# Image 1's backward convolution taps: from the vector engine to products with diagonal matrices on the tensor engine

## The chip, the cores and the metric

The kernel runs on one core of a Trainium2 chip. The metric is the device time of one execution in microseconds (us). A core has a tensor engine (PE in the profile, its weight loads PEld), a vector engine (DVE), a scalar engine (ACT), a general engine (POOL), a queue that issues all transfers here (SP), and 16 DMA engines. The engines run side by side, each through its own list of instructions in order, and wait for one another by semaphores. Everything is in fp32.

## The reference, cut to what matters

Two images of 48 x 48 tokens with 768 channels go through two residual layers. Layer 0 is attention of every token to its 7 x 7 neighbourhood. Layer 1 is a selective scan (Mamba) over the 2304 tokens of an image in both directions:

```
xz = X @ in_proj_w.T                                   # x and z, 1536 channels each
out_f = branch(xz, conv_w, conv_b, ...)                # forward
out_b = branch(xz reversed in time, conv_w_b, ...)     # backward, turned back afterwards
out = (out_f + out_b) @ out_proj_w.T

branch: x = silu(depthwise_conv(x, 4 taps) + conv_b)
        dt, B, C = x @ x_proj_w.T;  delta = softplus(dt @ dt_proj_w.T + b)
        h[t] = exp(delta[t] * A) * h[t-1] + delta[t] * x[t] * B[t]      # 16 states a channel
        y[t] = sum over states of h[t] * C[t] + x[t] * Dp;  result y * silu(z)
```

The depthwise convolution has four taps for each channel: a sum of four shifted copies of the channel's row, each times a number that belongs to the channel. The backward branch takes its taps from the other side, so both branches read the same projected row x, with three more tokens on each side.

## The kernel before, in words

**Layout.** Channels lie on the 128 partitions, time along the free dimension. The 2304 tokens are cut into 6 chunks of 384 (CHUNKS), the 1536 inner channels into ND = 12 blocks of 128. One block in one chunk in one direction is a *unit*; 12 units are a *pass*. There are 24 passes, 288 units: image 0 forward (passes 0 to 5), image 0 backward (6 to 11), image 1 forward (12 to 17), image 1 backward (18 to 23).

**A unit** (scan, from L1180) has four groups of four states. Per group: a product delta*x*B over 4 x 386 elements (L1225, tile hb), which the planner gives to DVE or to POOL for three of the four groups; four exponentials on ACT into PSUM (L1247, tile da); two scans on DVE of two states each (L1258); a product with C on POOL (L1273); transposing products on PE that add the states up (L1290, tile py). ACT then copies py to SBUF (L1316). So a unit has 8 scans and a pass has 96. Before a unit, deltas_of projects delta (L1151, L1157), takes the softplus (L1162), multiplies by Dp (L1170, ACT) and by x (L1175, POOL).

**The projections and the convolution** (in_proj, from L880). For each chunk the normalised inputs xc (six blocks of 128 channels, 390 tokens) are loaded. For each block k of the 1536, u_tile loads 384 KB of weights w_x and makes six products into a PSUM bank px (L382, called from product). From px both branches' convolutions are made, for back = 0 and back = 1: ACT writes the tap that has no shift with the bias (L928), DVE adds the other three taps one after the other (L935), all reading px in PSUM:

```
def tap(j, back=back, q=q, at=at):
    u = uz[:, back, kk, :cl]
    nc.vector.scalar_tensor_tensor(
        u, px[:, at[j] : at[j] + cl], q["conv_w"][:, k, j : j + 1], u,
        ALU.mult, ALU.add,
    )
```

Three blocks are collected in a tile uz, ACT applies silu to them (L961, with a table load ahead and behind), and they are stored. x_proj loads them again and makes dt, B and C.

**What lies beside what.** The attention of image 0 comes first. Its in_proj is spread over image 0's forward passes, the attention of image 1 over units 50 to 118, in_proj of image 1 from unit 118 on, 12 units to a chunk. Its z parts for the first four chunks and the output projections come later.

**What sets the order.** The program is not written out in order. Every piece of work is handed to a planner (class Order) with its engine, an estimated duration, a key (its place in the sequence of units), and the buffers that it reads and writes. The planner walks through time: each engine takes next the piece that can start first by those estimates; pieces of which a key lies over 2.5 units ahead of the oldest unfinished unit wait. Pieces of the scan rank by key, side work (job=True) may be put off where it would delay scans. Products of L1225 with an alternative (alt) go to whichever engine is free first. Where PE would stand idle for over 0.8 us between a unit's first and last transposes, the planner adds transposes of the identity (L1491, called *fillers* here) that nobody reads. Each engine then executes its list in the planned order, whatever the chip does.

**Buffers.** Tag "mm": 2 PSUM banks, shared by px, the delta, z, x_proj and output products and by the last transposes of a backward unit. Tag "w": 5 SBUF buffers for weights. Tag "ev": 4 buffers of 384 columns for copies out of PSUM. Tag "hb": 7 buffers. Loads and stores all go through the SP queue in planned order; a load that waits for its buffer holds up the ones behind it.

Of the kernel before, what the change touches and what calls it, by code (L numbers as in the profile page):

```python
# [48 lines left out]
CONV = 4  # L49
HALO = CONV - 1  # L50
NEG = -1e30

# [193 lines left out]
def tile_kernel(  # L246
# [56 lines left out]
    yg = spill("yg", [DI, L], ND * NCW)  # L303

    state = Buf("state", parts=ND * NSG, ap=res.tile([P, ND, 2 * NS + 1], F32, tag="state", name="state"))
    nc.gpsimd.memset(state.ap, 0.0)
# [15 lines left out]
    def ps(tag, n):  # L322
        return Buf(f"{tag}_{n}", psum, [P, 512], tag, BUFS.get(tag, 1))
# [48 lines left out]
    def product(acc, cl, w, x, key, m=P, job=True, o0=0, to=None, also=()):  # L372
# [4 lines left out]
        for c0 in range(0, n, 3):  # L377

            def part(c0=c0):
# [10 lines left out]
                "PE", mm(3, cl), part, key, [*used, *([] if first else [acc])],  # L390
                [acc, *([to] if first and to else [])], job=job,
            )

    def parameters(key):

        for i, (conv_w, conv_b, xpT, dtT, dt_b, A_log, Dp) in enumerate((fwd, bwd)):
# [18 lines left out]
            add("ACT", 800, decay, key + i + 0.5, r=[v], w=[v], job=True)  # L415
            pars.append(v)
        for j, t in enumerate(xd[0] + xd[1]):

            def unit(t=t):
                for l0, cl in CHUNKS:  # L420
                    nc.sync.dma_start(t.ap[RK : RK + 1, l0 : l0 + cl], ones[:, :cl])

            add("SP", 2400, unit, key + 2 + 0.1 * j, w=[t], job=True)
# [105 lines left out]
    def attention(b, start, end, job, T):  # L529
# [25 lines left out]
        def project(t):  # L555
# [18 lines left out]
            for p in range(NP):  # L574
                for s in range(2):
# [4 lines left out]
                    )  # L580
                    acc, e = ps("mm", f"qk{n}"), sb(turn("ev"), [P, TB], n)
                    product(
# [3 lines left out]
                    if s == 0:  # L586
# [3 lines left out]
                            lambda acc=acc, e=e: nc.scalar.mul(  # L590
                                e.ap.rearrange("p (u r c) -> p u r c", u=HW // QC, r=QR),
                                acc[:, :TB].rearrange("p (r u c) -> p u r c", u=HW // QC, r=QR),
# [5 lines left out]
                    else:  # L598
                        add(
                            "DVE", dve(TB),  # L600
                            lambda acc=acc, e=e: nc.vector.tensor_copy(e.ap, acc[:, :TB]),  # L601
                            key + 0.01, r=[acc], w=[e], **S,
# [4 lines left out]
                    add(  # L607
                        "SP", 400, lambda to=to, e=e: nc.sync.dma_start(to(), e.ap), key + 0.02,
                        r=[e], w=[dst], size=P * TB * 4, **S,
                    )  # L610
            for hf in range(NP // 3):
# [7 lines left out]
                for m in range(TB // P):  # L619
                    n = f"v{b}_{t}_{hf}_{m}"  # L620
                    acc, e = ps("mm", n), sb(turn("ev"), [P, TB], n)
                    for i in range(nw):
# [5 lines left out]
                    add(  # L628
                        "ACT", act(TB), lambda acc=acc, e=e: nc.scalar.copy(e.ap, acc[:, :TB]),
                        key + 0.01, r=[acc], w=[e], **S,  # L630
# [3 lines left out]
                        lambda e=e, m=m, hf=hf: nc.sync.dma_start(  # L634
                            vd[b][t * TB + m * P : t * TB + (m + 1) * P, hf * TB : (hf + 1) * TB], e.ap
                        ),
# [243 lines left out]
    def in_proj(b, i, start, end, conv=True, gate=True, nk=KB, tags=("uz",), banks=("mm",), proj=None):  # L880

        shift, rstd = norms[b]
        l0, cl = CHUNKS[i]
        lo, n = l0 - HALO, cl + 2 * HALO
# [32 lines left out]
        def u_tile(k, kk, nk, uz, key, bank):  # L917
            m = f"{b}_{i}_{k}"
            (wx,) = weights(w_inT, [(0, k * P)], f"x{m}", key, after=got)
            px = ps(bank, f"xin_{m}")  # L920
            product(px, n, [(wx, c, 0) for c in range(NC)], [(xc, c, 0) for c in range(NC)], key, to=uz)
            for back in (0, 1):
                q = par[back]
# [18 lines left out]
                for j in range(HALO):  # L942
                    add(
                        "DVE", dve(cl) + 70, lambda j=j, tap=tap: tap(j), key + 0.04, r=[px, part],
                        w=[part], job=True,
                    )

        def z_tile(k, kk, nk, uz, s, key):
# [83 lines left out]
    def xd_out(b, back, l0, cl, n, acc, key):  # L1032
        t = sb("ev", [P, TB], n)
        add(
# [507 lines left out]
```

## Time and profile before

| what | value |
|---|---|
| median of 6 runs | 7045.02 us (7034.2 to 7048.28) |
| the profiled execution | 7044.31 us; its span in the profile 7042.5 us |
| granted PE clock, mean | 0.978 |
| DMA | 1101.32 MB, mean 156 GB/s |
| L1258 DVE, scans | 2304, 3926.7 us busy |
| L1273 POOL, product with C | 1152, 3654.6 us |
| L1247 ACT, exponentials | 4608, 2677.1 us |
| L1290 PE, transposes | 13824, 1745.1 us |
| L935 DVE, taps, both images | 864 records; the 432 of image 1 between 4015 and 5105 us |
| L928 ACT, first tap with bias | 164.9 us for 264 records on the uz tiles |

How to read it: busy time is the time in which an engine executes; register and semaphore instructions are not counted. In a row of instruction groups stand the line, engine, operation, output tile <- input tiles, shapes and number, then busy us and mean ns of one, then the idle time just before these instructions and what ended most of it. Instructions of one engine can overlap, so busy time divided by the number can be below the mean of one. "uz_u<-mm_xin" is a tile of name uz_u written from a PSUM tile mm_xin. The 40 slices give tenths of busy time along the span. The chain is followed back from the last instruction to whatever released each step.

### The profile page before, as it was taken

The numbers are of one execution on the slowest core, as the hardware profiler recorded it, in microseconds if no ns is written. First come the engines' busy times: TensorE is split into PE (matmuls) and PEld (weight loads), VectorE is DVE, ScalarE is ACT, GpSimd is POOL, SyncE is SP. The second block draws the span as 40 slices with busy tenths as digits, with TensorE's granted clock in tenths as the row PEclk, the third lists the DMA queues.
The fourth block names the chain that finished last, engine by engine and source line by source line (L and its number), as shares of the span: only waits on it lengthen the run. The fifth ranks groups of instructions, "written<-read, shape, count | busy, mean of one in ns | idle before, by whom it ended". The sixth has DMA issues, their size and how long they took to land.

```text
span 7042.5 us, 105645 instructions
## 1 busy us (share of the span) xinstructions
PE 6316.5 (90%) x38151; PEld 4833.1 (69%) x38151; DVE 6062.6 (86%) x6217; ACT 4969.4 (71%) x10948; POOL 5447.3 (77%) x1951
## 2 busy tenths in 40 slices
PE   7999989989999999999988888888888898999888
PEld 5666656666666776676666656666688887777777
DVE  2354449999999999998998999999999999999998
ACT  1323248788888788887888778778876667777765
POOL 0000008888989999998898878999999999999997
PEclk9999989999999999999999999999999999999999
DMA  6565454445556444554444354343466676655553
GB/s 190 173 197 175 137 156 132 141 137 157 156 154 199 152 147 137 156 173 147 128 144 133 112 166 134 100 143 112 141 179 191 176 219 194 194 178 157 162 170 105
DMA packets 1337698, 1101.32 MB, mean 156 GB/s; under 512 B 136328, under 2 KB 1327416, under 8 KB 1337144
## 3 DMA queue, kind: packets, MB, share of 16 engines
q1 hardware_dynamic: 1337176, 1094.56, 51.9%
q8 instruction: 303, 4.96, 0.3%
q14 instruction: 219, 1.79, 0.1%
HBM read 881.41 MB, written 213.57 MB: 155 GB/s over the span
## 4 chain that ended last, share of the span: by engine, by line
DVE 39%; PE 19%; ACT 15%; POOL 13%; issue 9%; DMA 5%; SPq 1%; DVEq 0%; POOLq 0%; ACTq 0%
DVE hb L1258 26%; POOL hb L1273 8%; DVE hb L1225 7%; ACT da L1247 5%; PE mm_qk L382 4%; POOL hb L1225 4%; DVE uz_u L935 3%; PE mm_v L382 2%; PE mm_ao L382 2%; PE py L1290 2%; PE mm_xin L382 1%; ACT pr L785 1%; DMA bc<-xdb 1%; PE da L825 1%; ACT L1163 1%
## 5 line engine op out<-in xcount | busy, mean ns | idle before, releaser
L1258 DVE TENSOR_TENSOR_SCAN hb<-da,hb 128x772 f32<-128x772 f32 x2304 | 3926.7, 1748 | 179.8 <-ACT da L1247 146.3
L1273 POOL TENSOR_TENSOR hb<-hb,bc 128x1536 f32<-128x1536 f32 x1152 | 3654.6, 3188 | 370.6 <-DVE hb L1258 328.6
L1247 ACT ACTIVATE da<-dlt,A 128x384 f32<-128x384 f32 x4608 | 2677.1, 584 | 909.1 <-DVE hb L1258 838.8
L1290 PE MATMUL py<-ident,hb 128*128 128x128 f32 x13824 | 1745.1, 278 | 280.5 <-POOL hb L1273 273.0
L1290 PEld LDWEIGHTS py<-ident,hb 128*128 128x128 f32 x13824 | 1560.1, 143 | 541.4 <-POOL hb L1273 437.1
L1225 POOL TENSOR_TENSOR hb<-u,bc 128x1544 f32<-128x1544 f32 x495 | 1585.2, 3204 | 23.5 <-PE py L1290 16.9
L1225 DVE TENSOR_TENSOR hb<-du,bc 128x1544 f32<-128x1544 f32 x657 | 1142.2, 1744 | 33.5 <-ACT du L1202 25.0
L1175 POOL TENSOR_TENSOR u<-dlt,u 128x384 f32<-128x384 f32 x288 | 263.9, 918 | 529.4 <-ACT dlt L1162 417.3
L382 PE MATMUL mm_z<-xc,w_z 128*128 128x384 f32 x1728 | 607.1, 492 | 6.6 <-ACT dlt L1157 3.9
L382 PE MATMUL mm_xin<-xc,w_x 128*128 128x390 f32 x1656 | 586.0, 499 | 26.0 <-DVE uz_u L935 16.2
L382 PE MATMUL mm_out<-stage_y,w_o 128*128 128x192 f32 x3168 | 561.5, 332 | 16.7 <-ACT dlt L1157 6.4
L1491 PE MATMUL py<-ident 128*128 128x128 f32 x4431 | 548.3, 276 | 0.0
L382 PEld LDWEIGHTS mm_out<-stage_y,w_o 128*128 128x128 f32 x3168 | 522.8, 194 | 27.8 <-ACT dlt L1157 10.6
L1491 PEld LDWEIGHTS py<-ident 128*128 128x128 f32 x4431 | 501.2, 142 | 29.2 <-issue 26.4
L901 POOL MEMSET xc<- 128x18 f32 x4 | 0.5, 116 | 638.2 <-DVE sm L779 638.2
L935 DVE SCALAR_TENSOR_TENSOR uz_u<-mm_xin,conv_w,uz_u 128x384 f32<-128x384 f32 x792 | 428.3, 607 | 47.6 <-ACT uz_u L928 44.8
L382 PEld LDWEIGHTS mm_xin<-xc,w_x 128*128 128x128 f32 x1656 | 308.0, 193 | 234.9 <-issue 29.4
L382 PE MATMUL mm_qk<-xc_xn,w_qk 128*128 128x384 f32 x1296 | 454.1, 496 | 13.9 <-DVE ev L601 2.6
L382 PEld LDWEIGHTS mm_z<-xc,w_z 128*128 128x128 f32 x1728 | 315.2, 192 | 192.1 <-issue 8.2
L382 PEld LDWEIGHTS mm_qk<-xc_xn,w_qk 128*128 128x128 f32 x1296 | 238.8, 193 | 170.9 <-issue 17.2
L785 ACT ACTIVATE pr<-pr,sm 128x308 f32<-128x308 f32 x432 | 234.5, 544 | 126.9 <-DVE sm L779 126.6
L1306 PE MATMUL py<-ident,vt 128*128 128x128 f32 x864 | 154.3, 289 | 147.1 <-ACT yt L1316 146.8
(163 smaller groups left out, 6793.3 us busy)
## 6 DMA issues: line engine op xcount, KB each, us to landing
w_o<-in_w_opT SPq DMA_DIRECT2D x264, 384.0 KB
bc<-xdf SPq DMA_DIRECT2D x96, 768.0 KB
bc<-xdb SPq DMA_DIRECT2D x96, 768.0 KB
w_qk<-in_w_qkv SPq DMA_DIRECT2D x144, 384.0 KB
w_x<-in_w_inT SPq DMA_DIRECT2D x144, 384.0 KB
w_z<-in_w_inT SPq DMA_DIRECT2D x144, 384.0 KB
w_ao<-in_w_out SPq DMA_DIRECT2D x72, 384.0 KB
u<-uf SPq DMA_DIRECT2D x48, 576.0 KB
```

The costliest lines, as they stand in the source:

```text
L382: nc.tensor.matmul(acc[:m, o0 : o0 + cl], wb[:, wi, wo : wo + m], xb[:, xi, xo : xo + cl], start=c == 0, stop=c == n - 1,)
L785: nc.scalar.activation(pr[j].ap, pr[j].ap, AF.Exp, bias=sm[:, j : j + 1], scale=-1.0, accum_out=sm[:, 2 + j : 3 + j],)
L825: nc.tensor.transpose(bank(pt, 512 - P)[:nk, k * P : (k + 1) * P], pr[j][:, c0 : c0 + nk], ident,)
L935: nc.vector.scalar_tensor_tensor(u, px[:, at[j] : at[j] + cl], q["conv_w"][:, k, j : j + 1], u, ALU.mult, ALU.add,)
L1175: lambda j=j: nc.gpsimd.tensor_mul(u[:, j, h], dl[:, j, c], u[:, j, h]), at + 0.06 + 0.25 * j,
L1225: on.tensor_mul(cells(hb, SG), by.unsqueeze(1).to_broadcast([P, SG, W]), bc[g].ap)
L1247: lambda: nc.scalar.activation(cells(da, 2)[:, j % 2, h], dl[:, jd, c], AF.Exp, scale=q["A"][:, k, i : i + 1]),
L1258: lambda: nc.vector.tensor_tensor_scan(flip(hb[at2]), flip(da[:, : 2 * W]), flip(hb[at2]), 0.0, ALU.mult, ALU.add),
L1273: lambda: nc.gpsimd.tensor_mul(cells(hb, SG)[:, :, h], cells(hb, SG)[:, :, h], bc[NSG + g][:, :, c]),
L1290: nc.tensor.matmul(py[:tp, t * P : (t + 1) * P], cells(hb, SG)[:, j, h][:, tb[t]], ident, start=False, stop=g == NSG - 1 and j == SG - 1 a ...
L1306: nc.tensor.matmul(py[:tp, t * P : (t + 1) * P], vt[:, tb[t]], ident, start=t == 0, stop=False, is_transpose=True, skip_group_check=True,)
L1491: nc.tensor.matmul(marks["py"][:, CL : CL + P], ident, ident, start=False, stop=False, is_transpose=True, skip_group_check=True,)
```

## The change

For image 1 alone (head is false where b = 1) the three backward taps on DVE and the backward first tap on ACT are replaced.

- Once, early in image 0's attention: for each of the 12 blocks and 4 taps, POOL multiplies the 128 x 128 identity by the backward tap's column of numbers; the four diagonal matrices of a block (256 KB) are stored to a DRAM tensor taps.
- For each of the 72 tiles (6 chunks x 12 blocks) of image 1: the block's four diagonal matrices are loaded into a buffer with tag "w"; ACT copies px (390 columns) to SBUF (xs, tag "ev"); PE makes four products of a diagonal matrix with a shifted window of xs into a second "mm" bank; ACT copies the sum with the bias into uz.
- The forward convolution of image 1 and both of image 0 are left as they were.
- The "ev" buffers grow from 384 to 390 columns; their other users take the first 384.
- The lists of instructions are planned anew.

The diff, cut to its core:

```diff
+EV = CL + 2 * HALO
...
+    taps = Buf("taps", parts=ND, ap=dram.tile([ND, P, CONV, P], F32, tag="taps", name="taps"))
...
     def parameters(key):
...
+        for k in range(ND):
+
+            diag = sb("w", [P, CONV, P], f"diag{k}")
+
+            def spread(k=k, diag=diag):
+                for j in range(CONV):
+                    nc.gpsimd.tensor_scalar_mul(diag[:, j, :], ident, par[1]["conv_w"][:, k, j : j + 1])
+
+            add("POOL", 1000, spread, key + 4 + 0.01 * k, r=[pars[1]], w=[diag], job=True)
+            add(
+                "SP", 400, lambda k=k, diag=diag: nc.sync.dma_start(taps[k], diag.ap),
+                key + 4.5 + 0.01 * k, r=[diag], w=[(taps, k)], job=True, size=P * CONV * P * 4,
+            )
...
-                    acc, e = ps("mm", f"qk{n}"), sb(turn("ev"), [P, TB], n)
+                    acc, e = ps("mm", f"qk{n}"), sb(turn("ev"), [P, EV], n)
...
         def u_tile(k, kk, nk, uz, key, bank):
...
-            product(px, n, [(wx, c, 0) for c in range(NC)], [(xc, c, 0) for c in range(NC)], key, to=uz)
-            for back in (0, 1):
+            own = [] if head else [sb("ev", [P, EV], f"xs{m}")]
+            product(
+                px, n, [(wx, c, 0) for c in range(NC)], [(xc, c, 0) for c in range(NC)], key,
+                to=[uz, *own],
+            )
+            if not head:
+                by_taps(k, kk, nk, uz, key, m, px, own[0])
+            for back in (0, 1) if head else (0,):
...
+        def by_taps(k, kk, nk, uz, key, m, px, xs):
+
+            q, part = par[1], (uz, nk + kk)
+            tw = sb("w", [P, CONV, P], f"t{m}")
+            add(
+                "SP", 400, lambda: nc.sync.dma_start(tw.ap, taps[k]), key - 0.35, r=[(taps, k)], w=[tw],
+                job=True, size=P * CONV * P * 4, after=got,
+            )
+            add("ACT", act(n), lambda: nc.scalar.copy(xs[:, :n], px[:, :n]), key + 0.01, [px], [xs], job=True)
+            pb = ps("mm", f"tap_{m}")
+
+            def sums():
+                for j in range(CONV):
+                    at = HALO + HALO - j
+                    nc.tensor.matmul(
+                        pb[:, :cl], tw[:, j, :], xs[:, at : at + cl], start=j == 0, stop=j == HALO
+                    )
+
+            add("PE", mm(CONV, cl), sums, key + 0.03, [xs, tw], [pb, part], job=True)
+            add(
+                "ACT", act(cl, 1),
+                lambda: nc.scalar.activation(
+                    uz[:, 1, kk, :cl], pb[:, :cl], AF.Identity, bias=q["conv_b"][:, k : k + 1]
+                ),
+                key + 0.05, [pb], [part], job=True,
+            )
```

## The prediction

> **What bounds the kernel now.** I read the page first: shares, the 40 slices, the chain that ended last.
>
> ```profile
> PE 6316.5 (90%) x38151; PEld 4833.1 (69%) x38151; DVE 6062.6 (86%) x6217; ACT 4969.4 (71%) x10948; POOL 5447.3 (77%) x1951
> ...
> DVE  2354449999999999998998999999999999999998
> ...
> DVE 39%; PE 19%; ACT 15%; POOL 13%; issue 9%; DMA 5%; SPq 1%; DVEq 0%; POOLq 0%; ACTq 0%
> ```
>
> After the first 1000 us DVE is full in nearly every slice and holds most of the chain; the 86% is an average with that first part. So time that leaves DVE later on can move the end. The page does not say which engine is next, so I cut the span into stages. The 2304 scans of L1258 are 8 to a unit (one block of 128 channels in one chunk) and 96 to a pass (one chunk, 12 units); I cut at every 96th. The taps of image 1 run from 4015 to 5105 us, which are passes 11 to 15 (3879 to 5191). The rows below, from the busy time by stage, give start and end, length, then busy us of PE, PEld, DVE, ACT, POOL, then PE clock, DMA share, GB/s.
>
> ```profile
> 250.00:500.00 250.00, 243.29 (x1286) 162.91 (x1284) 106.78 (x387) 67.09 (x200) 0.00 (x0) 0.99 0.63 196
> 3073.00:3344.00 271.00, 251.21 (x1610) 188.55 (x1609) 238.82 (x232) 210.54 (x542) 227.45 (x82) 0.97 0.51 154
> 3879.00:4174.00 295.00, 257.55 (x1504) 189.78 (x1503) 276.78 (x310) 228.01 (x458) 250.39 (x89) 0.95 0.47 141
> 4174.00:4455.00 281.00, 234.84 (x1350) 177.60 (x1348) 267.87 (x249) 216.85 (x390) 239.08 (x86) 0.96 0.44 134
> 4455.00:4699.00 244.00, 209.87 (x1351) 164.85 (x1350) 238.92 (x193) 193.35 (x399) 237.90 (x85) 0.99 0.37 112
> 4699.00:4947.00 248.00, 215.90 (x1205) 157.35 (x1203) 243.33 (x195) 204.85 (x416) 231.48 (x84) 0.99 0.43 131
> 4947.00:5191.00 244.00, 212.17 (x1314) 170.01 (x1315) 232.70 (x182) 196.21 (x395) 230.50 (x83) 0.99 0.46 139
> 5416.00:6325.00 909.00, 815.88 (x5282) 719.42 (x5281) 877.67 (x615) 661.24 (x1376) 877.82 (x314) 0.97 0.66 192
> ```
>
> Three things are to be seen. Without taps (5416 to 6325, four passes of 227 us) DVE and POOL both stand at 96.6%: that is their ceiling here. In passes 11 to 15 DVE is at 94 to 98% and POOL at 85 to 98%. And in pass 8 (3073 to 3344), with attention in place of taps, DVE has fallen to 88%, POOL to 84%, while PE is at 92.7%: there PE is the limit. So PE can bind in this kernel well below 100%, and the change loads PE.
>
> **Part by part.** Durations come from these rows:
>
> ```profile
> L1225 POOL TENSOR_TENSOR hb<-u,bc 128x1544 f32<-128x1544 f32 x495 | 1585.2, 3204 | 23.5 <-PE py L1290 16.9
> L1225 DVE TENSOR_TENSOR hb<-du,bc 128x1544 f32<-128x1544 f32 x657 | 1142.2, 1744 | 33.5 <-ACT du L1202 25.0
> ...
> L382 PE MATMUL mm_xin<-xc,w_x 128*128 128x390 f32 x1656 | 586.0, 499 | 26.0 <-DVE uz_u L935 16.2
> ...
> L1491 PE MATMUL py<-ident 128*128 128x128 f32 x4431 | 548.3, 276 | 0.0
> ...
> L935 DVE SCALAR_TENSOR_TENSOR uz_u<-mm_xin,conv_w,uz_u 128x384 f32<-128x384 f32 x792 | 428.3, 607 | 47.6 <-ACT uz_u L928 44.8
> ```
>
> *Removed.* 72 tiles lose three taps each, 216 in all; busy 428.3/792 = 0.541 us each: 117 us off DVE.
>
> *Added on PE.* Four 128x384 products per tile. The chain has this piece:
>
> ```profile
> 4045.59 7.87 PE mm_xin L382 x24
> ```
>
> Two records make one fp32 product, so 12 products of 390 columns took 7.87 us, 0.656 us each; 384 columns, 0.646. 72 x 4 x 0.646 = 186 us.
>
> *Moved by the planner.* Comparing the two kernels' instruction orders, and counting by pass: POOL's order is the same up to unit 138, so up to about 4000 us the kernel is unchanged but for a reshuffle in the first attention stage. In passes 11 to 15 the filler transposes of L1491 fall from 1582 to 564, 0.124 us each: 126 us off PE. And 14 of L1225's products go from POOL (3.20 us) to DVE (1.74 us): 45 us off POOL, 24 back onto DVE. Net over the five passes: DVE -93, POOL -45 to -50, PE +60.
>
> *ACT.* Each tile swaps one L928 (164.9/264 = 0.62 us) for a copy (as L1157, 133.4/288 = 0.46) and a biased copy (as L1170, 174.2/288 = 0.60): +0.44 us, +31 us in all. ACT is at 79% (1039 of 1312); I cost it at nothing. Without that cover it is 31 us.
>
> *DMA.* 72 loads of 256 KB, 19 MB, over 1312 us: 14 GB/s on top of some 131, at a share of 0.37 to 0.47. Hidden under the projections, unless a w slot comes free late; the w_x loads, which have that same wait, hold PE up 3.5 us in the whole run. As much again is my upper bound, nothing the lower. The SP queue has slack there: it waits 250 us in this stretch for transposed outputs alone.
>
> *First stage.* 48 small POOL products where POOL is idle, 12 stores of 256 KB and 12 uses of a w slot, each between loads for attention. DMA stands at 0.63. PE is at 97% and sets the pace; the weights that it awaits can only come later, or, by the reshuffle, by luck earlier: -5 to +10 us. I take 0.
>
> *New waits.* The tap products wait on PE for the ACT copy of the projection. Behind them on PE are the transposes of L1290, which free the hb buffers that DVE and POOL fill. The copy on ACT stands among the exponentials of L1247, which wait in order for scans (in this stretch 219 times, 152 us, the longest 3.7 us). The biased copy waits on ACT for the taps; behind it are exponentials for the next scans. What covers PE's wait is the work placed between the projection and the taps: less than 2 us in 25 tiles of 72, mostly one group of 12 transposes.
>
> **The sum by pass.** I add the moved and new work to each pass's busy time (also the shift of projections, z, x_proj and delta products between passes, by 0.656, 0.70, 0.36 and 0.86 us a product, and of L1273's by 3.2):
>
> | change in pass | 11 | 12 | 13 | 14 | 15 |
> |---|---|---|---|---|---|
> | DVE taps | -60 | -66 | -30 | -39 | -21 |
> | PE tap products | 68 | 80 | 52 | 44 | 44 |
> | PE projection products | -36 | 24 | 12 | -9 | 9 |
> | PE fillers | -104 | -255 | -306 | -90 | -263 |
> | L1225 on DVE / on POOL | 2 / -2 | -1 / 1 | 6 / -6 | 3 / -3 | 4 / -4 |
>
> - Pass 11 (295): PE 258 - 36 x 0.656 + 68 x 0.646 - 104 x 0.124 + 1 = 266; DVE 277 - 33 + 4 = 248; POOL 244.
> - Pass 12 (281): PE 235 + 16 + 52 - 32 - 3 = 268; DVE 268 - 36 - 2 = 230; POOL 245.
> - Pass 13 (244): PE 210 + 8 + 34 - 38 - 3 = 211; DVE 239 - 16 + 10 = 233; POOL 212.
> - Pass 14 (248): PE 216 - 6 + 28 - 11 - 9 = 218; DVE 243 - 21 + 5 = 227; POOL 228.
> - Pass 15 (244): PE 212 + 6 + 28 - 33 + 7 = 220; DVE 233 - 12 + 7 = 228; POOL 208.
>
> In the last three passes DVE or POOL at 96.6%, or PE at 92.7%, give 241, 236 and 237: 22 us less than before. In passes 11 and 12 PE decides. At pass 8's share, 92.7%, they take 287 and 289: 1290 in all, 22 us saved. At the share of the first attention stage (243.29/250 = 97.3%) 273 and 275: 1262, 50 saved. If PE did not bind, DVE and POOL would give 257 and 254: 1225, 87 saved. Pass 8 resembles the stretch in having scans beside; the first stage resembles it in its long products. I take the middle of the two, 95%: 280 and 282, 1276, **36 us saved**. After unit 192 the order is also different, with equal counts; nothing says which way, I allow 15 us. Against the profiled execution's 7044.3 us (span 7042.5) that is 7008; the median of 7045.0 is the same within a us.
>
> A rule speaks against using that 92.7%: the Trainium skill, "Perfetto Trace Analysis", section "Identifying the Most-Contended Engine", says that matmul busy share is a poor measure of TensorE's distance from its limit, and to read the LDWEIGHTS busy share instead. By that reading PE has room (860 of 1312, 66%), and the saving would be 87 us. Pass 8 shows PEld at only 70% with DVE and POOL both slack, so the row decides here.
>
> **The rivals.**
>
> 1. *PE near its ceiling in two passes* (forecast): -36, from -22 to -50. For it: pass 8. Chance 0.42.
> 2. *PE has room; DVE keeps the bound*: -87, with the later order -102 to -72, about 6957. For it: PE's true idle time in passes 11 to 15 plus fillers is 182 + 191 = 373 us, and 186 fit. Against: pass 8. Chance 0.22.
> 3. *Within 14 us (0.2%, about what a measurement of this kernel can tell from no change)*: the stalls of the fourth case eat most of the gain; 7040. Chance 0.16.
> 4. *Slower: PE stalls in the 25 tiles with little cover.* A copy behind one exponential that waits for a scan comes up to 3.7 us late, and then PE, already full, holds up the transposes. 25 stalls of 1.45 us are 36 us, and cancel the gain: from there it is slower. At 3 us each, 75 - 36 = +39: 7083. For it: PE already waits 43 us on POOL and ACT at its transposes in passes 11 and 12. Against: the shortest gaps hold 1.5 us of transposes, the copy itself takes 0.46, and ACT's waits average 0.7 us. Chance 0.20.
>
> That DVE is not relieved is excluded by the order: 216 taps are gone from it.
>
> Faster: cases 1 and 2, 0.64; same 0.16; slower 0.20. The range takes in case 2 down to 99 us and 20 us of case 4: 6945 to 7065. Left out: 0.03 below, 0.14 above.
>
> **What would show it.** Right: L935's successor with 648 instead of 864 records; DVE in passes 11 and 12 below 93%, PE at 94 to 96%; the five passes 1276 us long; everything up to 3879 us and each pass after 5191 as before within a few us. Wrong: PE in those passes under 92% and the stretch at 1230 (case 2), or the tap products among PE's largest waits, on the ACT copy (case 4); or a first stage longer than now by over 10 us.

## The result and the profile after

The changed kernel is slower: 7061.99 us (median of 19 runs, 7044.48 to 7074.06) against 7047.28 for the kernel before (39 runs beside them), a ratio of 1.0020 [1.0014, 1.0026], some 15 us. The forecast was 36 us faster. The profiled execution took 7074.06 us, span 7072.2; it is the slowest of the 19, so the rows below hold some 12 us more than the median execution.

The page after, the same lines as were shown of before (shares, DVE's slices, the chain that ended last):

```profile
PE 6390.2 (90%) x37702; PEld 4840.2 (68%) x37702; DVE 5988.4 (85%) x6016; ACT 4990.7 (71%) x11020; POOL 5428.5 (77%) x1984
...
DVE  1354449999999999998898978899999999999998
...
DVE 37%; PE 21%; ACT 17%; POOL 10%; issue 9%; DMA 6%; SPq 1%; DVEq 0%; POOLq 0%; ACTq 0%
```

DVE's row now has a 7 and two 8s just behind the middle (4066 to 4597 us), where it had 9s, and the chain holds 2 points less of DVE and 3 less of POOL, 2 more each of PE and ACT. So DVE was relieved, and the time did not follow. Cut again at every 96th scan, with the columns as in the prediction (start and end, length, busy us of PE, PEld, DVE, ACT, POOL, then PE clock, DMA share, GB/s), passes 11 to 15 of the changed kernel and their sum:

```profile
3894.54:4209.53 314.99, 280.44 (x1518) 200.26 (x1517) 253.77 (x256) 231.44 (x472) 248.87 (x89) 0.96 0.47 144
4209.53:4482.31 272.78, 241.38 (x1206) 170.20 (x1205) 233.87 (x181) 219.75 (x402) 233.25 (x84) 0.97 0.45 139
4482.31:4728.90 246.59, 220.84 (x1209) 162.59 (x1208) 234.25 (x166) 198.35 (x418) 221.72 (x80) 0.97 0.45 139
4728.90:4976.77 247.87, 220.00 (x1153) 155.71 (x1152) 228.70 (x159) 207.95 (x421) 219.91 (x80) 0.99 0.46 142
4976.77:5222.32 245.55, 225.95 (x1159) 161.46 (x1158) 230.28 (x163) 203.57 (x415) 222.91 (x80) 0.99 0.47 143
3894.54:5222.32 1327.78, 1188.61 (x6236) 850.23 (x6235) 1180.87 (x921) 1061.05 (x2125) 1146.66 (x409) 0.97 0.46 141
```

The same stretch of the kernel before, as one row:

```profile
3879.10:5190.60 1311.50, 1129.83 (x6712) 859.20 (x6711) 1259.14 (x1124) 1038.80 (x2053) 1188.95 (x423) 0.97 0.43 132
```

The busy sums moved about as forecast: PE +59 us (forecast +60), DVE -78 (-93), POOL -42 (-45 to -50), ACT +22 (+31). The length did not: 1328 instead of the forecast 1276, and 16 us more than before. Pass 11 alone grew by 20. No engine stands at the 96.6% that the prediction took for the ceiling: DVE has fallen from 96.0% to 88.9%, POOL from 90.7% to 86.4%, and PE is at 89.5%. Outside the stretch nothing changed that counts: passes 16 on took 1813 us (1815 before); pass 11 starts 15 us later than in the run before, but up to there every kernel of this study has the same work in nearly the same order, and its start lies between 3876 and 3901 us.

The groups that answer to the rows of the prediction:

```profile
L1275 POOL TENSOR_TENSOR hb<-u,bc 128x1544 f32<-128x1544 f32 x480 | 1535.6, 3201 | 29.6 <-PE py L1340 23.9
L1275 DVE TENSOR_TENSOR hb<-du,bc 128x1544 f32<-128x1544 f32 x672 | 1168.2, 1745 | 66.1 <-ACT du L1252 51.1
...
L1541 PE MATMUL py<-ident 128*128 128x128 f32 x3406 | 427.3, 277 | 0.0
...
L958 DVE SCALAR_TENSOR_TENSOR uz_u<-mm_xin,conv_w,uz_u 128x384 f32<-128x384 f32 x576 | 326.3, 610 | 88.3 <-ACT uz_u L951 82.1
```

DVE's taps are 216 fewer (792 to 576 records of this form), yet the idle time ahead of them rose from 47.6 to 88.3 us, and ahead of the products on DVE from 33.5 to 66.1: DVE waits for ACT now. The waits in the stretch (waiting instruction <- what it waited for: us, times, longest), DVE's and then those at the new instructions of PE and ACT:

```profile
DVE uz_u L958 <- ACT uz_u L951: 46.4, 14, 12.9
DVE hb L1308 <- ACT da L1297: 40.8, 27, 5.4
DVE hb L1275 <- ACT du L1252: 21.9, 11, 4.7
```

```profile
PE mm_tap L985 <- ACT ev_xs L979: 12.3, 10, 2.2
```

```profile
ACT uz_u L992 <- PE mm_tap L985: 20.7, 16, 3.2
ACT ev_xs L979 <- PE mm_xin L385: 17.3, 12, 3.6
```

DVE's three were 10.5, 20.1 and 4.2 us before.

**The change of image.** Pass 12 is the first of image 1. Its first scan needs a chain: the group norm's end, twelve projections and convolutions of chunk 0, silu, a store, x_proj, a store, B and C back, delta. I measure it from the last DVE instruction on the norm's tiles to the first scan of pass 12: 175 us before (3999 to 4174), 194 after (4016 to 4210). Pieces of the chain that ended last, there, and POOL's wait at its end:

```profile
4161.15 2.58 PE mm_tap L985 x8
4163.74 1.31 PE py L1340 x12
4165.05 3.90 PE mm_xd L385 x24
4168.95 7.87 PE mm_xin L385 x24
4176.90 4.10 PE mm_xd L385 x24
4181.00 5.16 PE mm_tap L985 x16
```

```profile
POOL u L1225 <- DMA dtw<-dtT: 29.9, 1, 29.9
```

These pieces run over PE, the tap products stand among them, and POOL stands still for 30 us until delta is there. In every version here the norm ends 120 to 123 us after the start of pass 11; the rest of the pass is this chain.

### The profile page after: what moved, and what is told of

It reads as the page before. It is cut to its first block, busy times and chain, and to the rows that moved or that the text cites. A ratio compares the mean times of both kernels' runs of the same rounds, so it can differ in the third digit from the quotient of the medians.

```text
span 7072.2 us, 104795 instructions
## 1 busy us (share of the span) xinstructions
PE 6390.2 (90%) x37702; PEld 4840.2 (68%) x37702; DVE 5988.4 (85%) x6016; ACT 4990.7 (71%) x11020; POOL 5428.5 (77%) x1984
## 4 chain that ended last, share of the span: by engine, by line
DVE 37%; PE 21%; ACT 17%; POOL 10%; issue 9%; DMA 6%; SPq 1%; DVEq 0%; POOLq 0%; ACTq 0%
DVE hb L1308 25%; POOL hb L1323 7%; DVE hb L1275 6%; ACT da L1297 5%; PE mm_qk L385 4%; POOL hb L1275 3%; PE py L1340 3%; DVE uz_u L958 3%; PE mm_v L385 2%; PE mm_ao L385 2%; PE mm_out L385 1%; PE mm_xin L385 1%; ACT pr L801 1%; ACT pT L848 1%; ACT L1213 1%
## 5 line engine op out<-in xcount | busy, mean ns | idle before, releaser
L1275 POOL TENSOR_TENSOR hb<-u,bc 128x1544 f32<-128x1544 f32 x480 | 1535.6, 3201 | 29.6 <-PE py L1340 23.9
L1275 DVE TENSOR_TENSOR hb<-du,bc 128x1544 f32<-128x1544 f32 x672 | 1168.2, 1745 | 66.1 <-ACT du L1252 51.1
L1541 PE MATMUL py<-ident 128*128 128x128 f32 x3406 | 427.3, 277 | 0.0
L1541 PEld LDWEIGHTS py<-ident 128*128 128x128 f32 x3406 | 388.0, 143 | 29.6 <-issue 26.0
L958 DVE SCALAR_TENSOR_TENSOR uz_u<-mm_xin,conv_w,uz_u 128x384 f32<-128x384 f32 x576 | 326.3, 610 | 88.3 <-ACT uz_u L951 82.1
```

What stands on the lines that cost most here:

```text
L958: nc.vector.scalar_tensor_tensor(u, px[:, at[j] : at[j] + cl], q["conv_w"][:, k, j : j + 1], u, ALU.mult, ALU.add,)
L1275: on.tensor_mul(cells(hb, SG), by.unsqueeze(1).to_broadcast([P, SG, W]), bc[g].ap)
L1541: nc.tensor.matmul(marks["py"][:, CL : CL + P], ident, ident, start=False, stop=False, is_transpose=True, skip_group_check=True,)
```

## The experiments

The theories (TensorE, VectorE, ScalarE and GpSimd are PE, DVE, ACT and POOL). **Theory 1**, the prediction's: TensorE is near its ceiling, and its added work eats the relief. **Theory 4**, its fourth case: the copy on ScalarE is late. A **third**: the passes are not set by the busiest engine, but by chains through several engines, which run through their lists in order. Theories with letters are explained in the texts put down before the runs. This table has the ratio to the kernel before, the length of pass 11, the length of passes 12 to 15 together, and DVE's busy share in those four (from the rows by stage). All but the first line are explained below.

| kernel | ratio [95%] | pass 11 | 12 to 15 | DVE there |
|---|---|---|---|---|
| before | 1 | 295 | 1016 | 96.6% |
| after | 1.0020 [1.0014, 1.0026] | 315 | 1013 | 91.5% |
| e1, relief | 0.9953 [0.9938, 0.9968] | 296 | 978 | 94.5% |
| e6, relief and copy | 0.9951 [0.9935, 0.9966] | 291 | 990 | 93.3% |
| f1, relief and loads | 0.9921 [0.9906, 0.9936] | 288 | 976 | 94.9% |
| e2, one product run | 1.0029 [1.0018, 1.0041] | 310 | 1019 | 91.1% |
| e5, one run, one told | 1.0006 [0.9997, 1.0015] | 308 | 1005 | 92.0% |
| k1, four run, one told | 1.0096 [1.0082, 1.0110] | 326 | 1059 | 87.6% |
| e3, not in chunk 0 | 0.9992 [0.9983, 1.0001] | 298 | 1012 | 91.5% |
| w2, not in chunks 0, 1 | 0.9986 [0.9977, 0.9995] | 296 | 1006 | 93.7% |
| k2, w2 with one told | 1.0035 [1.0022, 1.0047] | 293 | 1043 | 89.5% |
| e7, no copy | 1.0014 [1.0005, 1.0023] | 295 | 1016 | 92.1% |
| f2, no loads | 1.0031 [1.0018, 1.0044] | 314 | 1006 | 92.2% |
| f3, f2 not in chunk 0 | 1.0037 [1.0023, 1.0051] | 297 | 1025 | 89.5% |
| h1, products unread | 1.0025 [1.0015, 1.0035] | 354 | 974 | 94.0% |
| h3, one unread | 0.9984 [0.9974, 0.9994] | 332 | 966 | 94.7% |
| h2, unread, from the copy | 1.0031 [1.0021, 1.0041] | 314 | 1022 | 91.5% |
| h5, same bank | 1.0040 [1.0026, 1.0053] | 326 | 1016 | 91.3% |
| e8, null | 1.0003 [0.9994, 1.0013] | 293 | 1023 | 96.1% |
| e4, taps from SBUF | 1.0331 [1.0314, 1.0348] | 348 | 1207 | |

Up to pass 11 and from pass 16 on the kernels differ too: passes 16 on took 1807 to 1833 us. So orders of like merit lie up to some 20 us apart there, and the two columns by stage say more than the ratio.

### The relief alone (e1), with the copy (e6), with the loads (f1)

e1, from the kernel before:

```diff
-                for j in range(HALO):
+                for j in range(0 if b and back else HALO):
```

> The kernel before, planned anew with the three backward taps of image 1 left out on DVE (216 of 864; part of the backward convolution is missing) and nothing put in their place. It measures what relieving DVE is worth by itself. If the tensor engine's new work ate the gain (theory 1), this one is 60 to 100 us faster than the kernel before, as the rival case of the prediction worked out (87 us). If other engines hold the passes at the same length anyway (theory 3), it is faster by under 30 us.

e6 adds to that, for image 1, an "ev" buffer and a ScalarE copy of px into it that nobody reads:

```diff
+            if b:
+                xs = sb("ev", [P, TB], f"xs{m}")
+                add("ACT", act(n), lambda: nc.scalar.copy(xs.ap, px[:, :TB]), key + 0.01, [px], [xs], job=True)
```

> The kernel before with the three backward taps of image 1 left out on DVE, as in the first experiment, plus one ACT copy of the projection to SBUF per tile that nobody reads (72 x 0.46 = 33 us of ACT work); no products, no loads, no second bank. Theory 4 (ACT's copies make the exponentials late that the scans wait for): most of the 35 us of relief is lost, 7040 or more. Otherwise it keeps at least 20 of them, 7020 to 7035.

f1 is the changed kernel without copy, second bank and products, its biased pass reading px; loads and "w" buffers stay:

```diff
-            add("ACT", act(n), lambda: nc.scalar.copy(xs[:, :n], px[:, :n]), ...)
-            pb = ps("mm", f"tap_{m}")
-            add("PE", mm(CONV, cl), sums, ...)
...
-                    uz[:, 1, kk, :cl], pb[:, :cl], AF.Identity, bias=q["conv_b"][:, k : k + 1]
+                    uz[:, 1, kk, :cl], px[:, HALO : HALO + cl], AF.Identity, bias=tw[:, 0, 0:1]
```

> Image 1's backward convolution is left out but for one ScalarE pass per tile straight from the projection's bank; of the change only the first stage's diagonal matrices, the 72 loads of them and their "w" slots are kept (no copy, no second bank, no product). Theory L (the loads take "w" slots and stand in SyncE's queue, where the profile after shows 116 us of waits of that line, so weights come late): 10 to 30 us of the 35 that the relief alone was worth are lost, ratio 0.997 to 0.9995. Theory B (the second PSUM bank of each tile and the longer chain through it, or the order made anew for them): all 35 us are kept, ratio 0.994 to 0.9965.

The relief, with nothing added, was worth 33 us by the ratio of e1, between the two ranges that were put down (60 to 100, and under 30); with the copy 35; with the loads 56. By the ratios neither the copy's work (theory 4) nor the loads (theory L) cost anything that shows. What it costs to wait for the copy e6 does not test: nobody reads it there. Pass 11 and passes 12 to 15 of e1, then of f1, then of e6, and POOL's wait for delta at the change of image in f1:

```profile
3891.30:4187.50 296.20, 263.82 (x1476) 193.04 (x1475) 257.67 (x263) 229.52 (x459) 244.28 (x87) 0.93 0.48 144
4187.50:5165.50 978.00, 850.26 (x5029) 653.38 (x5027) 924.02 (x660) 807.88 (x1598) 901.54 (x322) 0.97 0.44 133
```

```profile
3877.20:4165.60 288.40, 252.36 (x1450) 184.76 (x1448) 255.74 (x261) 226.06 (x458) 244.00 (x87) 0.95 0.53 161
4165.60:5141.10 975.50, 852.27 (x4999) 647.73 (x4999) 925.54 (x664) 803.53 (x1597) 895.93 (x321) 0.98 0.49 149
```

```profile
3891.40:4182.00 290.60, 253.65 (x1451) 184.17 (x1450) 260.13 (x265) 240.20 (x483) 240.49 (x86) 0.96 0.50 148
4182.00:5172.10 990.10, 850.26 (x5034) 647.39 (x5033) 924.25 (x659) 823.97 (x1643) 897.00 (x322) 0.98 0.43 131
```

```profile
POOL u L1213 <- ACT dlt L1200: 15.0, 1, 15.0
```

Pass 11 is the thing to see. It loses 20 us of DVE work (277 to 258, 256) and gets no shorter in e1, 7 us in f1: DVE falls from 94% to 87 or 89%. The chain of the image's start takes 173 and 167 us there, 175 before, and POOL waits for its end. The relief is won almost wholly in passes 12 to 15: 38 us in e1, 41 in f1, 26 in e6.

### Fewer products, and what the planner is told (e2, e5, k1)

e2 keeps the order of the changed kernel and runs one product of the four; e5 also tells the planner; k1 runs all four and tells the planner one:

```diff
-                for j in range(CONV):                    # e2, e5
+                for j in range(1):
...
-            add("PE", mm(CONV, cl), sums, ...            # e5, k1
+            add("PE", mm(1, cl), sums, ...
```

> The changed kernel with exactly its order of instructions, but one of the four products with diagonal matrices per tile (three taps of image 1's backward convolution are left out); copies, loads, buffers and waits stay. PE loses 72 x 3 x 0.646 = 140 us of work in the stretch. Theory 1 (PE is the limit there): the stretch of five passes gets 60 to 90 us shorter and the total about 60 to 80 below the changed kernel. Theory 2 (the two PSUM banks and the waits on copies are the limit): under 30 us shorter, since each tile still takes its second bank and its two copies.

> The changed kernel with one product of four per tile (three taps of image 1's backward convolution are left out), and this time the planner is told the shorter duration, so that the order is made anew. With the old order the same cut brought nothing (7073 us), so the length of the tap products does not act through the chip's PE any more; it can still act through the order. If the order had to be stretched to find PE room (theory 5), this one is 20 to 40 us below the changed kernel. If ACT's two copies (theory 4) or the second PSUM bank are what costs, it stays within 15 us of the changed kernel.

> All four products of a tile run on the chip, but the planner is told the length of one: the order of the run with one planned product, with the work of the changed kernel. Theory O (the loss sits in the order that the planner writes for TensorE's load, not in the time of the products on the chip): as that run, ratio 0.9995 to 1.0015, passes 11 to 15 of 1308 to 1322. Theory P (the products' own time on TensorE holds the others up, and the order made for four had hidden it): 15 us or more above that run, ratio 1.0025 or more, passes 11 to 15 above 1328.

In the stretch, with the order made for four, four products took 1328 us and one 1329 (e2's rows, pass 11 and the stretch, follow). With the order made for one, one took 1313 and four 1385. By the ratios e5 is 10 us faster than the changed kernel, less than theory 5's 20 to 40. Theory P held against theory O. Theory 1 fell as it was put (137 us of products fewer brought nothing), and a part of it came back: where the order has no room for the products, they cost.

```profile
3900.80:4211.14 310.34, 259.91 (x1414) 188.23 (x1413) 253.66 (x256) 231.22 (x472) 248.85 (x89) 0.92 0.48 146
3900.80:5229.59 1328.79, 1098.08 (x5800) 794.00 (x5799) 1181.01 (x922) 1060.60 (x2125) 1145.89 (x409) 0.94 0.47 141
```

The products and the fillers of e5 and then of k1, both over the stretch:

```profile
L1541 PE MATMUL py<-ident 128*128 128x128 f32 x1254 | 161.7, 283 | 0.0
...
L985 PE MATMUL mm_tap<-ev_xs,w_t 128*128 128x384 f32 x144 | 65.5, 540 | 38.7 <-ACT ev_xs L979 23.5 <-ACT da L1297 10.5 <-ACT dlt L1207 1.8
```

```profile
L985 PE MATMUL mm_tap<-ev_xs,w_t 128*128 128x384 f32 x576 | 204.9, 499 | 27.9 <-ACT ev_xs L979 18.4 <-ACT da L1297 6.6 <-ACT dlt L1207 1.1
L1541 PE MATMUL py<-ident 128*128 128x128 f32 x1254 | 157.1, 278 | 0.0
```

k1 has e5's order with its 1254 fillers, and 139 us more of products. In the changed kernel the planner had left 576 fillers of 1570: that is how it makes room. Without that, the delay goes over ScalarE, which comes to the biased copy before the products are done, and from there to DVE. ACT's and DVE's waits in k1; the same two were 11.4 and 61.0 us in e5:

```profile
ACT uz_u L992 <- PE mm_tap L985: 104.6, 63, 4.7
```

```profile
DVE hb L1308 <- ACT da L1297: 104.5, 49, 9.6
```

### The first chunks left out (e3, w2, k2)

```diff
-        head = not b
+        head = not b or i == 0        # e3
+        head = not b or i < 2         # w2, and k2 with mm(1, cl) told for four products
```

> The changed kernel with the change left out for chunk 0 of image 1 alone (12 of 72 tiles convolved on DVE as before), the rest by diagonal products. The trace of the changed kernel shows POOL idle for 30 us just before image 1's first scan, which waits for chunk 0's projections, x_proj and loads; these took 20 us longer than before the change. Theory 1: pass 11 loses its extra 20 us, total 15 to 25 us below the changed kernel, so about even with or a little below the kernel before. If the longer pass 11 was only the work of DVE and POOL put in another place: no gain, 0 to 5 us.

> The changed kernel with the change left out for chunks 0 and 1 of image 1 (24 of 72 tiles on DVE as before). Leaving it out for chunk 0 alone gave 7049 against 7054 for the kernel before in the same call. Chunk 1 is projected while the scans of the image change are late, so I expect a little more: 7035 to 7045, 5 to 15 us below the kernel before. If chunk 0 was the whole of what the start cost, it equals the first exemption, 0 to 5 below.

> The variant that leaves the change out for chunks 0 and 1 of image 1 (ratio 0.9986), with the planner told one product of the four. Theory O: the same or some 5 us better, ratio 0.9975 to 0.999. Theory P: 5 to 15 us worse, ratio 0.9993 to 1.001.

e3 takes chunk 0's copies, tap products and biased copies out of the chain of the image's start, and changes nothing else. That chain goes back to 176 us, pass 11 to 298, and passes 12 to 15 stay where they were: 18 us of the stretch, and 20 us by the ratios, sat in that one place.

```profile
3876.20:4173.70 297.50, 261.73 (x1504) 191.91 (x1503) 267.64 (x290) 226.72 (x459) 247.58 (x88) 0.96 0.47 142
4173.70:5186.00 1012.30, 915.18 (x4732) 653.89 (x4731) 925.98 (x665) 830.65 (x1655) 906.13 (x324) 0.97 0.46 141
```

Which of the three costs it is a second question, and the products' own time is the smaller part of the answer: in e2, with one product of four in the same order, the chain still takes 189 us (194 in the changed kernel), though with PE's clock at 0.92 in that pass. w2 is the best version that computes everything: 10 us below the kernel before, and its interval leaves out 1. k2, with no room for its products, is 35 us slower than w2, as k1 is 63 us slower than e5.

### No copy (e7), no loads (f2, f3)

e7 takes the products' input from the normalised input xc, which lies ready, in place of the copy; f2 takes the identity in place of the loaded matrices; f3 is f2 with chunk 0 left out:

```diff
-                        pb[:, :cl], tw[:, j, :], xs[:, at : at + cl], ...
+                        pb[:, :cl], tw[:, j, :], xc[:, 0, at : at + cl], ...      # e7; the copy goes
+                        pb[:, :cl], ident, xs[:, at : at + cl], ...               # f2, f3; the loads go
```

> The changed kernel without the ACT copy: the products with diagonal matrices read the normalised inputs xc, which lie in SBUF anyway, in place of the copy of the projection (so the backward convolution of image 1 is taken of other data). Products, loads, second bank and biased copy stay; ACT has 33 us less work and no tap product waits for a copy. Theory 4: 20 to 35 us below the changed kernel. If products and bank are what costs: within 15 us of it.

> The changed kernel without the 72 loads and their "w" slots: the four products of a tile take the identity matrix that is in SBUF, so image 1's backward convolution is computed with wrong taps. Copy, second bank, products and biased copy stay. Theory L: 10 to 30 us are gained against the changed kernel, ratio 0.997 to 1.000. Theory B: the time of the changed kernel, ratio 1.001 to 1.003.

> As the run without loads, and the change left out for chunk 0 of image 1. If the chain at the image's start (13 to 20 us) and the loads (theory L) are both causes and add up: ratio 0.994 to 0.9975. If the chain alone is (theory B): as with chunk 0 left out alone, ratio 0.998 to 1.0005.

Without the copy, PE no longer waits for it; pass 11 goes back to 295 and the chain to 173 us with all four products in place, but passes 12 to 15 stay at 1016, and ScalarE's waits for the products remain. From pass 16 on e7 was 15 us longer than the changed kernel; so the ratio hardly fell, by some 4 us, where theory 4 had 20 to 35. So at the image's start it is the way through the copy, or the order that the planner makes for it (in e7 15 tiles are projected ahead of pass 12, in the changed kernel 17), that costs more than the products. Without the loads nothing is gained, as f1 had it. f3 should have had the gain of e3 and did in pass 11 (297), but lost 19 us in passes 12 to 15 against f2 and 12 against e3. I have no cause for that but its order.

### Is it the waits, the second bank, or the work? (h1, h2, h3, h5)

h1: products from xc, and nobody reads them; h3: the same with one product, which the planner is told; h2: the changed kernel, with the biased pass reading px, so that the products wait for the copy and nobody for the products; h5: the products written into px after its last reader, no second bank:

```diff
-                    uz[:, 1, kk, :cl], pb[:, :cl], ...
+                    uz[:, 1, kk, :cl], px[:, HALO : HALO + cl], ...      # h1, h2, h3
...
-            pb = ps("mm", f"tap_{m}")
+            pb = px                                                      # h5, called after the DVE taps
```

> The relief with the loads and with the four products per tile, but nothing waits for the products: they read the normalised input, their bank is read by nobody, and the backward part of image 1 is one ScalarE pass straight from the projection's bank (its taps are left out). Read by the passes 13 to 15, which took 736 us before, 740 in the changed kernel, 716 and 717 with the relief alone and with the relief and the loads. Theory R (the round trip TensorE to ScalarE to TensorE to ScalarE of each tile, in queues that run in order): 714 to 722, ratio 0.992 to 0.996. Theory K (the second "mm" bank of each tile takes the double buffering from the projections): 732 or more, ratio 0.997 to 1.004. Theory P (TensorE's work, in the order made for it): the same as K.

> The changed kernel with one thing altered: the biased pass reads the projection's bank, not the products', so nothing waits for the products, which are made from the copy as before (image 1's backward taps are so left out). Theory R: only ScalarE's wait for the products is gone, so passes 13 to 15 take 716 to 730 and the ratio is 0.993 to 0.999. Theories K and P: 732 or more, ratio 0.998 to 1.004.

> As the run with unread products, with one product per tile, which the planner is told. Theory R: 714 to 720 in passes 13 to 15. Theory K: 732 or more, as with four. Theory P: a quarter of the loss, 718 to 724.

> The changed kernel with the four products written into the projection's own bank, after its last reader (the third forward tap), instead of into a second one. Theory K: the loss goes, passes 13 to 15 take 714 to 725, ratio 0.994 to 0.999. Theories R and P: 732 or more, ratio 1.000 to 1.004.

By the ratios this looked like theory P (TensorE's work): h1 is as slow as the changed kernel, h3 between. The stretch as a whole says the same (h1 1328 us, as the changed kernel; h3 1298). By stages it is less clear. h1's two rows, pass 11 and passes 12 to 15:

```profile
3901.30:4255.60 354.30, 323.71 (x1596) 219.72 (x1595) 270.09 (x278) 241.49 (x475) 238.80 (x85) 0.96 0.48 144
4255.60:5229.10 973.50, 877.35 (x4758) 637.69 (x4757) 915.30 (x648) 791.35 (x1580) 897.40 (x322) 0.98 0.47 141
```

In h1 and h3 the planner put 24 tiles, two whole chunks, ahead of the first scan of image 1 (18 in f1, 17 in the changed kernel): 288 projection records there against 216 and 204. Pass 11 pays for that, and passes 12 to 15 have 10 us less of DVE work. Even so, DVE's share in those four is that of the relief alone (94.0 and 94.7%), with all four products per tile and PE at 90.1%. In h2, where PE waits for the copy again, it is 91.5%, as in the changed kernel. In e7, where only ScalarE waits for the products, 92.1%. So in passes 12 to 15 all versions in which nothing new waits stand at 93.3 to 94.9% (e1, e6, f1, h1, h3), and all with one of the two waits or both for every tile there at 87.6 to 92.2%. That speaks for theory R, weakly: h1 is the only version with four products and no new wait, six or seven tiles fewer stand in these passes there, and w2, with both waits for 48 tiles, has 93.7%. h5 speaks against the second bank (theory K): without it nothing is better. But there the projection's bank is held longer in its place.

For passes 13 to 15 alone, which the expectations go by, h1 took 729 us and h3 721, between relief (716, 717 and 731 for f1, e1, e6) and the changed kernel (740); h2 738, h5 750. Measured so, theory R missed: it had 714 to 722 for h1, 716 to 730 for h2 and 714 to 720 for h3, where theory P had 732 or more, 732 or more and 718 to 724 and came in for h2 and h3. The sorting by DVE's share was chosen only after these runs. So between waits and work in passes 12 to 15 nothing is decided.

### How much is the order itself? (e8)

```diff
-                        "DVE", dve(cl) + 70, lambda j=j, tap=tap: tap(j), ...
+                        "DVE", dve(cl) + (71 if b else 70), lambda j=j, tap=tap: tap(j), ...
```

> The kernel before with one number of the planner changed: image 1's taps are told as 71 ns longer than a plain VectorE operation instead of 70. No instruction is added or removed; the order of the work is made anew from image 1 on. Theory N (every new order costs or brings some ten microseconds by chance): ratio outside 0.999 to 1.001. Otherwise 0.9993 to 1.0007, and the differences of the other runs have causes of their own.

No difference by the ratio; theory N fell as it was put. This new order cost nothing; but where work is added or taken away the orders differ by more than this, as f3 and the spread from pass 16 on show.

### The forward taps from the copy (e4)

Image 1's forward convolution (the first tap on ACT, three on DVE) reads the SBUF copy instead of PSUM, so that px would come free sooner:

```diff
-                q = par[back]
+                q, px = par[back], px if head else own[0]
```

> The changed kernel, but image 1's forward convolution (the first tap on ACT and three on DVE) reads the copy in SBUF instead of the PSUM bank, so the bank is free after one ACT copy instead of after three DVE taps. Theory 2 (banks): 20 to 50 us faster than the changed kernel. Theory 1 (PE): within 10 us of it.

3.3% slower, for a reason that has nothing to do with this question; it is told at the end.

## Why the prediction was wrong, point by point

- **The counts were right.** 216 taps off DVE, PE +59 us, ACT +22, fewer fillers (1570 to 576 records, 191 to 73 us: -118 for -126 forecast). The products took 200 us for 186.
- **ACT and DMA at nothing: right** as far as their own time goes (e6 and f1 keep the relief), and so was the first stage (pass 0 starts at 1056.6 us, before 1057.6). After 5191 us the order brought nothing, as forecast.
- **The step that failed is the sum by pass**: a pass was given the busy time of its fullest engine, divided by a ceiling. It missed by 52 us: 35 in pass 11 (280 forecast, 315 measured), 17 in passes 12 to 15 (282 + 241 + 236 + 237 = 996 forecast, 1013 measured). The ceilings were no ceilings: the prediction's own rows have DVE at 98% in passes 13 and 14, above the 96.6%, and that PE was the limit of pass 8 was read from its share alone; no run tested it.
- *In pass 11* the ceiling was the wrong model for both kernels. Its length is some 120 us up to the end of the group norm, where no tap stands, and then the chain to image 1's first scan. Taking 20 us of DVE work out of it shortened it by 0 to 7 us (e1, e6, f1: 288 to 296, where DVE's and POOL's ceilings gave 257), and the change lengthened the chain by 19 (175 to 194). e3 shows where that sits: without the change in chunk 0 alone, pass 11 is at 298. It is not mainly the products' time on PE: with one of four (e2) the chain is 189, with all four and no copy (e7) 173. Whether the waits on the way through the copy cost it or the order made for them stays open. Of the 15 us of gain there at most 7 were to be had, and 20 of loss were not in the sum. The profile of before had a sign of it: in pass 11 no engine stood at its ceiling (DVE 94%, PE 87%, POOL 85%).
- *In passes 12 to 15* the ceilings of DVE and POOL gave 254 + 241 + 236 + 237 = 968 without a limit from PE in pass 12; relief alone took 976 to 990, 1 to 2% more, so that part held. The price of the products was 28 us in the sum (pass 12 at 95% of PE), and measured 23 to 37 (1012.8 less 990.1 to 975.5). The size was near, the reason as given was not: PE stands at 89.7% there, under every ceiling named, and running fewer products in the same order changed nothing (e2). Two causes remain: the two new waits, PE for the copy and ScalarE for the products, in lists that run in order; and the products' time through the order that is made for it. DVE's shares point to the first, the lengths of passes 13 to 15 in h1 to h3 to the second. It is not settled: each version has an order of its own, and h1 has six tiles fewer in these passes than f1, seven fewer than the changed kernel.
- **Case 4** had the right sign and a part of the mechanism. PE's wait for the copy is 12.3 us in all (10 times, longest 2.2), a third of the 36 us from which it was to decide; so its sign came out mostly for another reason, the chain of pass 11. The mirror image, ScalarE waiting for the products with exponentials behind it, was named under the new waits and never priced: 20.7 us, and 104.6 in k1.
- **Case 2**, PE has room: the stretch was to take 1230 us or so. Even with no products at all it took 1264 to 1281. So the 87 us were not there, for reasons that, as far as the waits show, lie with DVE's side: pass 11, and ScalarE's exponentials, for which DVE waited 20.1 us before and 37.0 in e1. As to the rule of the Trainium skill that was weighed there ("Perfetto Trace Analysis", "Identifying the Most-Contended Engine", which names the LDWEIGHTS share together with MFU, the share of peak arithmetic): by the LDWEIGHTS share alone, 64% in the changed kernel, PE had room, and the 87 us did not come; nor did the matmul share decide. At 89.5% matmul busy, the changed kernel did not mind 91 us less of it (e2), and k1, at 91.5%, was 72 us longer than e5 for 115 us more.
- **The signs to look for**: DVE below 93% in passes 11 and 12 came (81 and 86%); PE at 94 to 96% did not (89 and 88%); the stretch was neither 1276 nor 1230.

## What to carry to other kernels

A stage's length is the busiest engine's time over a ceiling only where that engine has work to do all the time; where a stage holds a chain that must end before anything behind it starts (an image change, a first chunk), price what a change puts into that chain, and expect little from relief beside it. Work that is moved to an engine with room still brings waits in both directions, and in lists that run in order each is passed on to whoever stands behind; look at both ends of each. Where a planner orders the work, tell it the true length of what is added: here the same four products cost 57 us more in the stretch (1385 against 1328) when it was told a quarter of their length.

## What the runs showed of the hardware that was not expected

**VectorE with two inputs in SBUF beside a busy GpSimd.** In e4 the forward taps of image 1 read the copy in SBUF and uz in SBUF. Part of that stretch (4300 to 5300 us), DVE's groups and then POOL's:

```profile
L958 DVE SCALAR_TENSOR_TENSOR uz_u<-ev_xs,conv_w,uz_u 128x384 f32<-128x384 f32 x134 | 255.3, 1906 | 19.3 <-ACT uz_u L951 15.5
```

```profile
L1323 POOL TENSOR_TENSOR hb<-hb,bc 128x1536 f32<-128x1536 f32 x159 | 510.7, 3219 | 203.5 <-DVE hb L1308 186.6 <-issue 5.9 <-PE mm_dl L1201 3.5
```

The same operation takes 610 ns with one input in PSUM, and 1906 here; POOL's products take 3219 instead of 3185. The Trainium skill, "SBUF — State Buffer", section "Who interferes with whom", says that a VectorE instruction with two SBUF inputs contends with a GpSimd instruction that reads SBUF, through a read interface that they share. The trace agrees: 1.3 us more for each tap, beside POOL instructions of 3.2 us. Taken one by one, 95 of the run's 216 forward taps of image 1 started while POOL executed nothing and took 616 ns; the 121 others took 2593 on average, and nearly all of them ended 411 to 420 ns after the POOL instruction that they had met. So the tap stood still until that instruction was over. In the changed kernel, with px in PSUM, the same taps took 614 ns beside POOL and 612 without. A copy out of PSUM so that the bank comes free sooner is thus no free gift to VectorE here.

**In e2 TensorE gave a part of the saving back in its clock.** e2 runs 432 product records fewer than the changed kernel, 137 us of them (200.5 to 63.1); PE's busy time in the stretch fell by 91. The granted clock there is 0.94 (0.92 in pass 11) against 0.97, over the whole run 0.968 to 0.972 in its six runs against 0.975 to 0.980, and the projections and transposes, the same instructions, took longer. The projections in the changed kernel and in e2:

```profile
L385 PE MATMUL mm_xin<-xc,w_x 128*128 128x390 f32 x864 | 305.7, 500 | 4.8 <-ACT dlt L1207 2.8 <-ACT uz_u L992 1.1 <-DVE uz_u L958 0.5
```

```profile
L385 PE MATMUL mm_xin<-xc,w_x 128*128 128x390 f32 x864 | 317.6, 514 | 14.7 <-ACT uz_u L992 4.6 <-ACT da L1297 3.1 <-ACT dlt L1207 3.0
```

So e2 tested the relief of PE with 91 us, not 137; it still brought nothing.
